# A second Strassen level in the fourth product of six projections

## The chip, the core and the metric

The kernel runs on one core of one Trainium2 chip. The metric is the device time of the launch in microseconds. The times below are of single executions; the profile is of one further execution, taken by the hardware profiler. Engines are named as the profile names them: PE (TensorE, matmuls), PEld (its weight loads), DVE (VectorE), ACT (ScalarE), POOL (GpSimd), SP (SyncE, which issues all DMAs here).

## What is computed

Four graph-attention layers over 128 graphs of 64 nodes with 512 features, all in float32. Each layer normalizes its input, applies a ReLU and adds the result of an attention whose mask is an adjacency matrix that all graphs share:

```python
h = jnp.maximum(_layernorm(x, axis=-1), 0.0)
x = x + layer(h)
# layer 0: softmax(q k^T / 8 + mask) v, q, k, v = h @ W + b, 8 heads of 64
# layer 1: the same, then @ Wo + bo
# layer 2: one head; (adj^T * (q k^T)), rows divided by their norm, times v; no bias
# layer 3: as layer 1 with one w_qkv, a projection w_proj, and o + layernorm(o) at its end
```

Nearly all of the arithmetic is in products of a 512x512 weight matrix with a block of activations.

## The kernel before

The 8192 rows (128 graphs x 64 nodes) are cut into 16 blocks of 512 rows (`T`), so each projection of a block is a product of two 512x512 matrices. The layers run one after another, and inside a layer the blocks. A block of layer 0 has three projections (q, k, v), of layer 1 four (q, k, v and the output projection o), of layer 2 two (two weight matrices are first folded into one by `fold`), of layer 3 four. The o projection of a block runs at the end of the next block (`pending`, `project`), when its attention is done.

**A projection.** Each one uses Strassen's form in Winograd's variant: the matrices are cut into 2x2 blocks of 256x256, and 7 block products stand for 8. `projection` (line 533) runs the products in the order of `ORDER` (line 44: 1, 6, 5, 2, 7, 3, 4). A product is four matmuls with a 128x128 stationary operand and 256 moving columns (`prod_T` for transposed results, with the weights stationary; `prod_N` with the activations stationary). A matmul of the code is two instructions in the trace[...]. The products accumulate in three PSUM banks of 512 columns (1 and 2; 6 and 7; 5 and 3), and product 4 has a bank of its own. Between products ACT and DVE copy parts out: `s1` (product 1), `u2` and `u3` (products 6 and 7 plus `s1`), `z5`. The four quarters of the result are written by:

- Y11: ACT copies the bank of products 1 and 2.
- Y12: DVE adds the bank of 5 and 3 to `u2`.
- Y22: POOL adds `u3` and `z5`.
- Y21: DVE adds the bank of product 4 to `u3`; with a bias it does so in two halves.

For the o projection of layer 1 (`emit_out1`) the residual rows `xo` take the place of `u2` and `u3`; POOL adds these into `xo`, and DVE adds the banks.

**Sums.** The sums of the activations' blocks that the products need (`S` for q, k and v; `SO` for o) are four additions of 128x512 on POOL (`sums_x`, line 501), for the very first block on DVE. The sums of the weights' blocks (`sums_w`) are made once for each weight matrix, on POOL, those of k0 on DVE.

**Attention.** `attend` issues the scores of a block (trace: so<-kT,qT) as one group of 64x64 matmuls, adds masks and takes maxima on DVE, subtracts on POOL, exponentiates on ACT, sums on DVE, normalizes on POOL, and transposes the weights by DVE copy, DMA transpose and ACT copy (tiles z, hp, s). Then follows the product with v (so<-s,v in layers 1 and 3, so<-v,s in layer 0), whose result goes in layer 1 to `oT` by DVE, from which `SO` is summed.

**The order of work.** The kernel records all operations first. `Plan` notes what each reads and writes and a duration for it (`duration`), and `order` (line 133) then makes a fixed order for each engine by list scheduling: each engine takes the ready step with the lowest rank, which is the order of recording. All products of a group (`plan.begin` to `plan.end`) stay together. Recording itself interleaves the work: projections are generators that stop after each product, and at each stop (`tick`) the due generators for attention, normalization, loads and stores go on by one step. So a product group is also the unit of time by which `yield` counts. All recorded instructions are issued from one line (L193 in the trace). On the chip each engine works through its own fixed list and waits where an input isn't there.

The buffers that the change touches: PSUM has four banks for the projections (`ps_mm`, trace: mm) and two tiles for attention (`ps_so`, trace: so), each handed out in turn by `Ring`; the weight tiles `w` hold 7 blocks of 256x256 for a matrix, four matrices at a time.

Of the kernel before, what the change touches and what calls it, by code (L numbers as in the profile page):

```python
# [18 lines left out]
P = 128  # L19
G = 64  # L20
# [23 lines left out]
ORDER = (1, 6, 5, 2, 7, 3, 4)  # L44
ORDER0 = (1, 2, 5, 6, 3, 7, 4)
# [172 lines left out]

PORT = 150.5
RUSH = 60  # L220
# [39 lines left out]
def gnn_stack_kernel(  # L260
# [26 lines left out]
    ps_mm = pool("ps_mm", 4, space=bass.MemoryType.PSUM)  # L287
    ps_so = pool("ps_so", 2, space=bass.MemoryType.PSUM)
# [10 lines left out]
    pw = ps_mm.tile([P, KC, P], F32, tag="mm", name="pw")  # L299
# [41 lines left out]

    def load_w(name, src):

        w = wp.tile([P, 7, 2, H2], F32, tag="w", name=name)


        def part(i, j):
            return src[i * H2 : (i + 1) * H2, j * H2 : (j + 1) * H2].rearrange("(c p) f -> p c f", p=P)

        dma(w[:, W11], part(0, 0))  # L350
        dma(w[:, W21], part(1, 0))
        dma(w[:, WT3], part(0, 1))
        dma(w[:, W22], part(1, 1))
        return w

    def sums_w(w, eng):
        tt = eng.tensor_tensor
        tt(w[:, WT1], w[:, WT3], w[:, W11], ALU.subtract)
        tt(w[:, WT2], w[:, W22], w[:, WT1], ALU.subtract)
        yield 1  # L360
        tt(w[:, WT4], w[:, W21], w[:, WT2], ALU.subtract)
        tt(w[:, WT3], w[:, W22], w[:, WT3], ALU.subtract)

    W = {}

    def weight(name, src, eng=gps):
        W[name] = load_w(name, src)
        yield 4
        yield from sums_w(W[name], eng)
# [27 lines left out]
    def raw(tag, src, nm):  # L397
        t = p1.tile([P, KC, D], F32, tag=tag, name=nm)
        for c in range(KC):
            dma(t[:, c, :], src[c * P : (c + 1) * P, :])  # L400
            yield 3
        return t

    def fold():

        rq = yield from raw("oT", wq2, "rq")
        rk = yield from raw("SO", wk2, "rk")
        yield 4
        for dc in range(KC):
            pa = ps_mm.tile([P, D], F32, tag="mm", name=f"pfa_{dc}")  # L410
            plan.begin()
            for ec in range(KC):
                pe.matmul(pa, rq[:, ec, ts(dc, P)], rk[:, ec, :], start=(ec == 0), stop=(ec == KC - 1))
            plan.end()
            f = p4.tile([P, D], F32, tag="z", name=f"fa_{dc}")
            act.copy(f, pa)
            yield 1
            dma(a2d[dc * P : (dc + 1) * P, :], f)
            yield 1
        rv = yield from raw("oT", wv2, "rv")  # L420
        yield 4
        for ec in range(KC):
            f = p4.tile([P, KC, P], F32, tag="z", name=f"ft_{ec}")
            turn(f, rv[:, ec, :], f"v2_{ec}")
            yield 1
            dma(v2d.rearrange("(c p) e -> p c e", p=P)[:, :, ts(ec, P)], f)
            yield 1
# [17 lines left out]
    hTs, Ss, vs = {}, {}, {}  # L445
    ready = set()
# [12 lines left out]
    def layer_norm(n):  # L459
        mv = sm.tile([P, NT, 2], F32, tag="mv", name=f"mv_{n}")  # L460
        rs = sm.tile([P, NT], F32, tag="rs", name=f"rs_{n}")
        nb = sm.tile([P, NT], F32, tag="nb", name=f"nb_{n}")

        def scales(at):
            pow_mhalf(rs[:, at], mv[:, at, 1], LN_EPS, f"{n}")
            dve.scalar_tensor_tensor(nb[:, at], mv[:, at, 0], -1.0, rs[:, at], ALU.mult, ALU.mult)

        for t in range(NT):
            stats(mv, t, xins[n][t], f"{n}")
            if n == 0:  # L470
                scales(slice(t, t + 1))
            if t % 2:
                yield 1
        if n:
            scales(slice(0, NT))
        yield 2
        hT = p2.tile([P, KC, T], F32, tag="hT", name=f"hT_{n}")
        hTs[n] = hT
        if n == 0:
            for t in range(NT):  # L480
                z = xins[n][t]
                act.activation(z, z, AF.Relu, bias=nb[:, t : t + 1], scale=rs[:, t : t + 1])
                pt = ps_mm.tile([P, KC, P], F32, tag="mm", name=f"pz_{n}_{t}")
                plan.begin()
                for c in range(KC):
                    pe.transpose(pt[:, c, :], z[:, ts(c, P)], ident)
                plan.end()
                if t == 1:
                    for i in range(WARM // 2):
                        pe.transpose(pw[:, i % KC, :], xins[n][0][:, ts(i % KC, P)], ident)  # L490
                (dve.tensor_copy if t else act.copy)(hT[:, :, ts(t, P)], pt)
        for t in range(NT) if n else ():
            z = xins[n][t]
            act.activation(z, z, AF.Relu, bias=nb[:, t : t + 1], scale=rs[:, t : t + 1])
            turn(hT[:, :, ts(t, P)], z, f"{n}_{t}")
            yield 1
        del xins[n]
        ready.add(("h", n))
        sums_of(n)

    def sums_x(tag, src, nm, eng):
        S = (p2 if tag == "S" else p1).tile([P, 4, 2, H2], F32, tag=tag, name=nm)
        x11, x12, x21, x22 = halves(src)
        tt = eng.tensor_tensor
        tt(S[:, 0], x21, x22, ALU.add)
        tt(S[:, 1], S[:, 0], x11, ALU.subtract)
        tt(S[:, 2], x11, x21, ALU.subtract)
        tt(S[:, 3], x12, S[:, 1], ALU.subtract)
        return {1: x11, 2: x12, 3: S[:, 3], 4: x22, 5: S[:, 0], 6: S[:, 1], 7: S[:, 2]}
# [19 lines left out]

    def projection(prod, w, xop, nm, emit, order=ORDER):  # L530

# [3 lines left out]
        def bank(i):  # L535
            banks[i] = ps_mm.tile([P, D], F32, tag="mm", name=f"pp{i}_{nm}")
            return banks[i]
# [5 lines left out]
        X = {1: 1, 2: 1, 6: 6, 7: 6, 5: 5, 3: 5, 4: 4}  # L543
        for i in order:
# [4 lines left out]
            prod(ps, w[:, BLOCKS[i]], xop()[i], first)  # L549
# [10 lines left out]
            elif i == 7:  # L560
                dve.tensor_tensor(tmp_tile("u3"), ps, tmp["s1"], ALU.add)
                emit("u3", tmp["u3"])
                emit("Y22", tmp["u3"], tmp["z5"])
            elif i == 4:
                emit("Y21", ps, tmp["u3"])
            elif i == 3:
                emit("Y12", ps, tmp["u2"])
            if i != order[-1]:
# [4 lines left out]
    def emit_plain(region):  # L573

        def emit(what, a, b=None):
# [15 lines left out]
    def emit_bias(region, bias):  # L591

        def emit(what, a, b=None):
# [37 lines left out]
    def scores(qT, kT, g, nm):  # L631
# [3 lines left out]
        pss = ps_so.tile([P, 2, 2, KC, G], F32, tag="so", name=f"pss_{nm}")  # L635
# [10 lines left out]
    def attend(n, qT, kT, v, done):  # L646
# [7 lines left out]
        for s, pss in zip(ss, psss):  # L654
            for b in range(2):
# [3 lines left out]
                )  # L659
            sf = s.rearrange("p q b j -> p (q b) j")  # L660
# [16 lines left out]
        for s in ss:  # L677
            aT = s.rearrange("p (q c) b j -> p q c (b j)", q=2)
            aTs.append(aT)
            for p in range(2):  # L680
                if n < N - 1:
                    turn(aT[:, p], s[:, p * KC : (p + 1) * KC].rearrange("p c b j -> p (c b j)"), f"a_{n}_{p}")
                else:
                    pt = ps_mm.tile([P, KC, P], F32, tag="mm", name=f"pa_{n}_{p}")
# [4 lines left out]
                    act.copy(aT[:, p], pt)  # L689
                yield 1  # L690
# [41 lines left out]
    def finish0(n):  # L732
        def done(aTs, v):
# [5 lines left out]
            for g, aT in enumerate(aTs):  # L739
                po = ps_so.tile([P, 2, 2, H2], F32, tag="so", name=f"po_{n}_{g}")  # L740
# [13 lines left out]
            for g, po in enumerate(pos):  # L754
                for j in range(2):
                    xv = xos[n][:, 2 * g : 2 * g + 2, j * H2 : (j + 1) * H2]
                    dve.tensor_tensor(xv, po[:, j], xv, ALU.add)
            yield 1
# [5 lines left out]
    def finish13(n):  # L764
        def done(aTs, v):
# [5 lines left out]
            for g, aT in enumerate(aTs):  # L771
                po = ps_so.tile([P, 2, 2, KC, G], F32, tag="so", name=f"po_{n}_{g}")
# [12 lines left out]
            for g, po in enumerate(pos):  # L785
                for b in range(2):
# [5 lines left out]
                    else:  # L792
                        act.copy(at, po[:, b])
            if n < N - 1:
                yield 1
                SOs[n] = sums_x("SO", oTs[n], f"SO_{n}", gps)
        return done

    def emit_out1(n):
# [3 lines left out]
        def emit(what, a, b=None):  # L803
# [18 lines left out]
    def emit_out3(n, o):  # L822
# [6 lines left out]
        def emit(what, a, b=None):  # L829
# [43 lines left out]
    def relate(n, hT=None, gT=None):  # L873


        prt = ps_mm.tile([P, D], F32, tag="mm", name=f"pr_{n}")
# [5 lines left out]
        if old:  # L882
# [6 lines left out]
            for g in range(2):  # L889
                po = ps_so.tile([P, 2, 2, H2], F32, tag="so", name=f"pv_{m}_{g}")  # L890
# [30 lines left out]
        if hT is not None:  # L921
            dve.tensor_tensor(rel, pr, adj2.unsqueeze(1).to_broadcast([P, NT, G]), ALU.mult)
            act.activation(sq, rel, AF.Square)
        yield 1
        if old:
            for t in range(NT):
                for j in range(2):
# [3 lines left out]
                    )  # L931
                yield t % 2
# [26 lines left out]
    def sums_of(n):  # L959
        assert ("h", n) in ready  # L960
        Ss[n] = sums_x("S", hTs[n], f"S_{n}", dve if n == 0 else gps)
# [3 lines left out]
    for name, got in zip(("q0", "k0"), first):  # L965
        W[name] = got
        now(sums_w(got, gps if name == "q0" else dve))
# [20 lines left out]
    def project(n):  # L988
# [5 lines left out]
        if m // NB == 1:  # L994
            run(projection(prod_N, W["o1"], sop, f"o_{m}", emit_out1(m)))
# [3 lines left out]
        else:  # L999
# [5 lines left out]
            run(projection(prod_N, W["o3"], sop, f"o_{m}", emit_out3(m, o)))  # L1005
            spawn(tail3(m, o))

    for n in range(N):
# [15 lines left out]
        if l != 2:  # L1024
            qT = p1.tile([P, KC, T], F32, tag="qT", name=f"qT_{n}")
            q_emit = emit_bias(region_T(qT), (bqc0, bqc1)[l]) if l < 2 else emit_plain(region_T(qT))
            run(projection(prod_T, W[f"q{l}"], xop, f"q_{n}", q_emit, ORDER if n else ORDER0))
# [4 lines left out]
            run(projection(prod_T, W[f"k{l}"], xop, f"k_{n}", k_emit))  # L1032
# [9 lines left out]
            run(projection(prod_N, W[f"v{l}"], xop, f"v_{n}", emit_plain(region_N(v))))  # L1042
# [3 lines left out]
        else:  # L1046
            gT = p1.tile([P, KC, T], F32, tag="qT", name=f"gT_{n}")
            run(projection(prod_T, W["a2"], xop, f"g_{n}", emit_plain(region_T(gT))))
# [5 lines left out]
            run(projection(prod_N, W["v2"], xop, f"v_{n}", emit_plain(region_N(v))))  # L1054
# [14 lines left out]
    for t in range(NT):  # L1069
        ps = ps_mm.tile([P, D], F32, tag="mm", name=f"pl_{t}")  # L1070
# [10 lines left out]
        dve.tensor_tensor(o, ps, R["bp"], ALU.add)  # L1081
        stats(mv, t, o, "last")
# [42 lines left out]
```

## Time and profile before

| | us |
|---|---|
| median of 3 runs | 2844.2 (2843.95 to 2844.62) |
| the profiled execution | 2844.57 |
| its span, first to last instruction | 2842.8 |

Shares of the stages, from the view of busy times by window:

| stage, us | PE | DVE | ACT | POOL |
|---|---|---|---|---|
| layer 0, 60 to 720 | 660.00 | 503.50 | 344.62 | 408.56 |
| layer 1, 740 to 1540 | 799.39 | 547.16 | 339.81 | 548.38 |

In a group's line of the profile stand line, engine, operation, output and inputs by the program's names (moving and stationary operand after the arrow), partitions and elements, the count, then the busy time in us and the mean duration in ns, then idle time before it and what ended that. Matmul records overlap: an instruction's record runs from its start to its last result, so spacing is read from the starts in the timeline. Each block of layer 1 takes 52.79 us (its scores start at 1063.42 us in one block and at 1169.01 us two blocks later).

### The profile page before, as it was taken

Reading aid. Unit: us, or ns where it says so; the run is one execution under the profiler, and the core shown is the slowest. Engines: PE = TensorE matmul, PEld = TensorE weight load, DVE = VectorE, ACT = ScalarE, POOL = GpSimd, SP = SyncE. Lnnn points to the kernel's source line nnn. Section 1 sums busy time; section 2 is a strip of 40 time slices with the busy share of each in tenths; the row PEclk is TensorE's granted clock in tenths of the full one; section 3 lists DMA queues with packets and bytes.
Section 4 is the critical chain, followed back from the end, with each engine's and each line's share of the span. In section 5 each row is a group of like instructions: output and inputs, shape, how many; then the busy total and the mean of one; then the engine's idle time right before and its main releaser. Section 6 shows DMA issues by size and latency. Waiting matters only on the chain.

```text
span 2842.8 us, 62036 instructions
## 1 busy us (share of the span) xinstructions
PE 2828.4 (99%) x25833; PEld 2471.6 (87%) x25833; DVE 2037.6 (72%) x3104; ACT 1248.0 (44%) x1589; POOL 1840.5 (65%) x1349
## 2 busy tenths in 40 slices
PE   9999999999999999999999999999999999999998
PEld 8878888888888888888888888888888888888887
DVE  7767778876767767667666555555688888778787
ACT  4555555454443534534434343443444444444442
POOL 6555566656766667667677334344678687787796
PEclk9999999999999999999999999999999999999999
DMA  6766666556453533533546565756433433433432
GB/s 158 163 137 156 143 146 134 127 128 163 105 120 80 124 95 82 131 85 86 136 114 156 136 162 143 164 128 157 120 86 94 119 86 95 112 91 96 109 84 66
DMA packets 634890, 342.29 MB, mean 120 GB/s; under 512 B 485232, under 2 KB 566384, under 8 KB 634608
## 3 DMA queue, kind: packets, MB, share of 16 engines
q1 hardware_dynamic: 634608, 338.32, 50.0%
q8 instruction: 202, 3.31, 0.5%
q14 instruction: 80, 0.66, 0.1%
HBM read 152.61 MB, written 69.21 MB: 78 GB/s over the span
## 4 chain that ended last, share of the span: by engine, by line
PE 96%; DVE 3%; issue 0%; POOL 0%; DMA 0%; ACT 0%; POOLq 0%; SPq 0%; DVEq 0%
PE mm L193 88%; PE so L193 8%; DVE z L193 1%; DVE st L193 0%; POOL s L193 0%; DVE u L193 0%; DVE sr L193 0%; DVE kT L193 0%; DMA xin<-in_x_dram 0%; DVE mv L193 0%; DVE w L193 0%; DVE xo L193 0%; ACT xin L193 0%; ACT oT L193 0%; POOLq L1120 0%
## 5 line engine op out<-in xcount | busy, mean ns | idle before, releaser
L193 PE MATMUL mm<-S,w 128*128 128x256 f32 x3584 | 817.2, 380 | 0.0
L193 PEld LDWEIGHTS mm<-S,w 128*128 128x128 f32 x3584 | 679.3, 190 | 93.8 <-issue 1.0
L193 PE MATMUL mm<-hT,w 128*128 128x256 f32 x2688 | 629.9, 380 | 4.0 <-DVE kT L193 3.7
L193 DVE TENSOR_TENSOR u<-mm,s 128x512 f32<-128x512 f32 x414 | 284.9, 688 | 480.1 <-PE mm L193 342.3
L193 PEld LDWEIGHTS mm<-hT,w 128*128 128x128 f32 x2688 | 509.6, 190 | 75.5 <-DVE kT L193 5.3
L193 PE MATMUL mm<-w,S 128*128 128x256 f32 x2048 | 472.8, 381 | 0.0
L193 PEld LDWEIGHTS mm<-w,S 128*128 128x128 f32 x2048 | 385.5, 190 | 53.8 <-issue 0.5
L193 ACT COPY hT<-hp 128x1024 uint16<-128x1024 uint16 x252 | 332.7, 1350 | 90.3 <-DMA hp<-z 90.2
L193 PE MATMUL mm<-w,hT 128*128 128x256 f32 x1536 | 366.4, 381 | 0.0
L193 ACT COPY s<-hp 128x1024 uint16<-128x1024 uint16 x188 | 252.3, 1352 | 204.3 <-DMA hp<-z 197.1
L193 ACT COPY s<-mm 128x512 f32<-128x512 f32 x211 | 123.0, 583 | 490.0 <-PE mm L193 419.0
L193 POOL TENSOR_TENSOR s<-s,mx 128x1024 f32<-128x1024 f32 x96 | 183.3, 1911 | 226.9 <-DVE mx L193 224.9
L193 PEld LDWEIGHTS mm<-w,hT 128*128 128x128 f32 x1536 | 289.2, 190 | 40.2 <-DVE v L193 0.2
L193 POOL TENSOR_TENSOR xo<-xo,row 128x512 f32<-128x512 f32 x192 | 286.1, 1510 | 8.4 <-DMA xo<-in_x_dram 5.7
L193 DVE COPY z<-s 128x1024 uint16<-128x1024 uint16 x188 | 278.2, 1501 | 6.7 <-POOL s L193 6.6
L193 DVE COPY z<-xin 128x1024 uint16<-128x1024 uint16 x252 | 245.3, 988 | 37.6 <-ACT xin L193 34.0
L193 ACT ACTIVATE xin<-xin,nb,rs 128x512 f32<-128x512 f32 x256 | 195.4, 808 | 90.5 <-DVE nb L193 89.9
L193 PE MATMUL mm<-w,SO 128*128 128x256 f32 x992 | 224.3, 379 | 0.0
L193 POOL TENSOR_TENSOR qT<-u,z 128x512 f32<-128x512 f32 x64 | 87.5, 1367 | 202.2 <-DVE u L193 189.8
L193 PEld LDWEIGHTS mm<-w,SO 128*128 128x128 f32 x992 | 188.5, 190 | 25.6
L193 POOL TENSOR_TENSOR s<-s,sr 128x1024 f32<-128x1024 f32 x96 | 187.3, 1963 | 34.2 <-DVE sr L193 32.1
L193 ACT ACTIVATE s<-s 128x1024 f32<-128x1024 f32 (+1 forms) x112 | 108.1, 966 | 200.3 <-POOL s L193 144.3
(98 smaller groups left out, 3667.7 us busy)
## 6 DMA issues: line engine op xcount, KB each, us to landing
xin<-x SPq DMA_DIRECT2D x192, 256.0 KB, 4.0
xo<-x SPq DMA_DIRECT2D x64, 512.0 KB, 4.5
xin<-in_x_dram SPq DMA_DIRECT2D x64, 256.0 KB, 3.2
x<-xo SPq DMA_DIRECT2D x64, 256.0 KB, 2.5
x<-xo SPq DMA_DIRECT2D x128, 128.0 KB, 2.5
x<-xo SPq DMA_DIRECT2D x32, 512.0 KB, 3.0
out_dram<-xo SPq DMA_DIRECT2D x30, 512.0 KB, 3.0
xo<-in_x_dram SPq DMA_DIRECT2D x32, 256.0 KB, 3.2
```

What stands on the lines that cost most here:

```text
L193: getattr(getattr(self.nc, eng), op)(*a, **k)
```

## The change

Product 4 multiplies the two blocks x22 and `WT4` as they are. In six projections (`LEVEL2`: k0 and v0 of layer 0, q1, k1, v1 and o1 of layer 1) it is now made by the same form once more: the 256x256 blocks are cut into 2x2 quarters of 128x128, and seven products of one 128x128 by 128x128 matmul stand for four of 128x256. They come in two groups, "4a" (four matmuls) and "4b" (three), in one bank, with the order of products 1, 6, 5, 4a, 2, 7, 3, 4b.

What belongs to it:

- `sums_x` makes four more sums of 128x128 where needed, into the place of x21, which nothing reads any more; `sums_w` makes four more for each of the six weight matrices, for which the weight tile is longer by 3 x 128 columns.
- After 4a ACT copies two quarters into a new tile `q` and DVE adds one; after 4b DVE adds another, and `close_2` writes the result with three POOL additions and two DVE ones, in place of the one addition of Y21.
- PSUM banks are now given and taken by name, in the order in which they come free (`Pool`), in place of the fixed turn of `Ring`. `fold` waits in recording until a bank is free, its loads are spread out (a stop of 12 for 3), and two stops in it are gone.

```diff
+FINER = (1, 6, 5, "4a", 2, 7, 3, "4b")
+LEVEL2 = {"k0", "v0", "q1", "k1", "v1", "o1"}
...
-    ps_mm = pool("ps_mm", 4, space=bass.MemoryType.PSUM)
-    ps_so = pool("ps_so", 2, space=bass.MemoryType.PSUM)
+    mm = ctx.enter_context(tc.tile_pool(name="ps_mm", bufs=1, space=bass.MemoryType.PSUM))
+    mm = Pool([mm.tile([P, D], F32, tag=f"mm_{i}", name=f"mm_{i}") for i in range(4)])
...
-        w = wp.tile([P, 7, 2, H2], F32, tag="w", name=name)
+        t = wp.tile([P, 7 * 2 * H2 + 3 * P], F32, tag="w", name=name)
...
+        t, e = w[:, WT4], W2[name]
+        if finer(name):
+            tt(e[:, 0], t[:, 0, P:], t[:, 0, :P], ALU.subtract)
+            tt(e[:, 1], t[:, 1, P:], e[:, 0], ALU.subtract)
+            yield 1
+            tt(e[:, 2], t[:, 1, :P], e[:, 1], ALU.subtract)
+            tt(t[:, 0, P:], t[:, 1, P:], t[:, 0, P:], ALU.subtract)
...
-            yield 3
+            yield 12
...
+        a, b, c, d = [x22[:, j, ts(i, P)] for i in range(2) for j in range(2)]
+        F = [x21[:, j, ts(i, P)] for i in range(2) for j in range(2)]
+        if needs2:
+            tt(F[0], c, d, ALU.add)
+            tt(F[1], F[0], a, ALU.subtract)
+            tt(F[2], a, c, ALU.subtract)
+            tt(F[3], b, F[1], ALU.subtract)
...
+    def prod_2(prod, ps, name, xop, todo):
...
+        at = {1: (0, 0), 2: (0, 0), 5: (0, 1), 3: (0, 1), 6: (1, 1), 7: (1, 1), 4: (1, 0)}
+        for i in todo:
+            x, out = xop["quarters"][i], quarter(ps, prod, *at[i])
+            a, b = (ws[i], x) if prod is prod_T else (x, ws[i])
+            pe.matmul(out, a, b, start=i == 1, stop=True, skip_group_check=True)
...
+    def close_2(prod, ps, q, base, dst, bias):
+        u2, u3, z5 = q[:, 1], q[:, 2], q[:, 3]
+        y12 = quarter(base, prod, 0, 1)
+        gps.tensor_tensor(y12, y12, u2, ALU.add)
+        y2 = base[:, :, P:] if prod is prod_T else base[:, 1, :].rearrange("p (v f) -> p v f", v=2)
+        gps.tensor_tensor(y2, y2, u3.unsqueeze(1).to_broadcast([P, 2, P]), ALU.add)
+        gps.tensor_tensor(dst[:, 1, P:], base[:, 1, P:], z5, ALU.add)
+        for at in ((slice(None), 0, slice(None)), (slice(None), 1, slice(0, P))):
+            if bias is None:
+                dve.tensor_tensor(dst[at], ps[at], base[at], ALU.add)
+            else:
+                dve.scalar_tensor_tensor(dst[at], ps[at], bias[at[1]], base[at], ALU.add, ALU.add)
...
+            elif i == "4a":
+                q = p1.tile([P, 4, P], F32, tag="q", name=f"q_{nm}")
+                act.copy(q[:, 0], quarter(pv, prod, 0, 0))
+                dst, base, bias = emit("close")
+                if bias is None:
+                    act.copy(q[:, 3], quarter(pv, prod, 0, 1))
+                else:
+                    act.activation(q[:, 3], quarter(pv, prod, 0, 1), AF.Identity, bias=bias[1])
+                dve.tensor_tensor(q[:, 1], quarter(pv, prod, 1, 1), q[:, 0], ALU.add)
+            elif i == "4b":
+                dve.tensor_tensor(q[:, 2], quarter(pv, prod, 1, 1), q[:, 0], ALU.add)
+                if base is None:
+                    base = tmp["u3"].rearrange("p (u v) -> p u v", u=2)
+                close_2(prod, pv, q, base, dst, bias)
```

## The prediction, made before the changed kernel ran

> **What bounds the kernel now.** I read the page's busy times and its chain first, then the matmul groups, then one block of the timeline.
>
> ```profile
> PE 2828.4 (99%) x25833; PEld 2471.6 (87%) x25833; DVE 2037.6 (72%) x3104; ACT 1248.0 (44%) x1589; POOL 1840.5 (65%) x1349
> ...
> PE 96%; DVE 3%; issue 0%; POOL 0%; DMA 0%; ACT 0%; POOLq 0%; SPq 0%; DVEq 0%
> ...
> L193 PE MATMUL mm<-hT,w 128*128 128x256 f32 x2688 | 629.9, 380 | 4.0 <-DVE kT L193 3.7
> L193 PEld LDWEIGHTS mm<-hT,w 128*128 128x128 f32 x2688 | 509.6, 190 | 75.5 <-DVE kT L193 5.3
> ```
>
> TensorE is on the chain for 96% of the span and hardly waits. Only PE time, or a new PE wait, can move the end. Inside layer 1 (740 to 1540 us) PE is busy 799.39 of 800 us, POOL 548.38, DVE 547.16: POOL has room, but not much.
>
> The timeline gives the true rate, as records overlap:
>
> ```profile
> 407.44 3.62 PE L193 MATMUL mm<-S,w 128*128 128x256 f32 x16
> ...
> 1565.55 2.08 PE L193 MATMUL mm<-qT,hT 128*64 128x64 f32 x64
> ```
>
> Sixteen 256-wide instructions last 3.62 us, the last one 0.38 alone: (3.62-0.38)/15 = 0.216 us each. A matmul of the code is two instructions, so a product of four is 8 x 0.216 = 1.726 us. In the second line, 64-column weights and 64-wide operands alternate between two halves of the array: (2.08-0.22)/63 = 29.5 ns, 59 ns per half.
>
> **What the Trainium skill says.** "TensorE: Matmul & The Clock Gate", section LDWEIGHTS: a load costs its columns / 1.2 GHz, 107 ns for 128. The trace agrees: after a pause at 12.1 us the first matmul's record is 483 ns where the others are 379, so it stood 104 ns behind its own load. Its section Back-to-back issue gap gives matmul streams with a load each a larger spacing at N=128 than the operand alone takes (81 ns for 56); no run here shows that for float32. "GPSIMD Engine Reference", section 3.1: a two-input add of 2048 takes 4497 ns, about 2.6 cycles an element, and section 1: its SBUF interfaces are shared with VectorE. The trace agrees with both:
>
> ```profile
> L193 POOL TENSOR_TENSOR xo<-xo,row x192: 1257/1712/1827, 34.9 to 2822.9; 128x512 f32<-128x512 f32 x192
> ...
> L193 POOL TENSOR_TENSOR S<-hT x126: 1254/1270/1731, 52.7 to 2748.6; 128x512 f32<-128x512 f32 x126
> ```
>
> Undisturbed 1.257 us for 512, and 1.71 when it meets VectorE.
>
> **The PE part.** The fourth product of six projections (k0, v0 in layer 0; q1, k1, v1, o1 in layer 1), 16 blocks each, is 96 products. Four 256-wide matmuls become seven 128-wide, 8 instructions become 14, each with its own load of 128 columns. The operand takes half of 256 wide: the 64-wide stream scaled up is 2 x 53 + 5 = 112 ns (59 ns is 53 of streaming and 5 beside), and the 104 ns load just fits behind it, as the 64-column loads already do behind 64-wide operands. So 14 x 0.112 = 1.568 us for 1.726: 0.158 us each, 96 x 0.158 = **15.2 us gained**. Bounds: 109 ns (half of 216 and nothing more) gains 19; at 123 ns (1.726/14) nothing is left; if loads blocked each other for their recorded 190 ns, 14 x 0.19 = 2.66 us would cost 90 us in all. The 59 ns stream speaks against that, since its loads are recorded at 138 ns and still don't space it.
>
> **VectorE and ScalarE.** The last add of the quarter (one of 512 wide at 685 ns, or two with bias at 478) becomes two 128-wide adds, one 256 and one 128. From 425 ns for 256 and 685 for 512 a 128-wide one is about 295: 295 x 2 + 425 + 295 = 1.31 us, so 0.46 to 0.63 us more. ScalarE gains two 128-wide copies, about 0.41 each (583 for 512, 471 for 256). In a layer-1 block of 52.8 us that is 2.2 us on VectorE (68% busy) and 3.3 us on ScalarE (42%). Both fit beside PE: cost 0, unless an add stands where PE waits for it (below).
>
> **POOL.** Each closing adds three operations (128, 256, 128 wide), and each sum of a layer-0 or layer-1 block, and of o1's input, four of 128. The trace has none so narrow. From 1.257 at 512 and 4.497 at 2048: 2.11 ns an element and 0.18 fixed, so 0.45 us for 128, 0.72 for 256. From below 0.31 (a quarter of 1.257), from above 0.90 (with the 0.45 that meeting VectorE adds). Per layer-1 block: 8 x 0.45 + 4 x 1.62 = 10.1 us, which takes POOL from 548/800 of 52.8 = 36.2 to 46.3 of 52.2 us, 89%. In layer 0, 1.8 + 3.24 = 5 us on top of 62%: room enough.
>
> **Where POOL meets PE.** The layer-1 block before:
>
> ```profile
> 1146.07 2.09 PE L193 MATMUL so<-s,v 64*64 64x64 f32 x128
> ...
> 1169.01 2.10 PE L193 MATMUL so<-kT,qT 64*64 64x64 f32 x128
> ```
> ```profile
> 1151.74 1.28 POOL L193 TENSOR_TENSOR SO<-oT 128x512 f32<-128x512 f32 x1 [3.06 <-DVE oT L193]
> 1153.10 1.27 POOL L193 TENSOR_TENSOR SO<-SO,oT 128x512 f32<-128x512 f32 x1
> ...
> 1161.80 1.26 POOL L193 TENSOR_TENSOR kT<-u,z 128x512 f32<-128x512 f32 x1
> ```
>
> After the attention product (so<-s,v) VectorE writes oT, POOL sums SO and S and then finishes k at 1163.1; scores start at 1169.0, so 5.9 us are spare. In the changed order of instructions scores stand after five products of v instead of three, and k's last part is now written by POOL, behind SO, its four small sums, S, four more, and its own closing. From the start of so<-s,v: PE needs 2.2 + 0.67 (rest of q's fourth) + six products 10.36 + 1.57 + five 8.63 = 23.4, and 1.05 more before the half of scores that reads the late part: 24.5 us. POOL: oT done 6.4 (5.67 before, and a small closing op now stands between its parts); SO 5.03, small 1.8, S 5.03, small 1.8, k 1.26, closing 1.62; nine handoffs between dependent small operations at 0.13 (1.36 between the starts above, where independent ones have 1.23) 1.2; 0.1 to PE: 24.2. Spare: 0.3 us.
>
> The other half, scores to the next so<-s,v: the last ScalarE copy of the weights ended at 1143.54, 27.4 us after that block's scores (1169.01 - 52.79 = 1116.22). A 1.7 us residual addition now stands before the second normalization on POOL: about +1.5, 28.9. PE arrives after 2.2 + 26.5 = 28.7. Spare: -0.2.
>
> Both are even to within about 1 us. What is queued behind such a wait is all of PE. I take **0.3 us a block, 15 blocks, 4.5 us lost**; bounds 0 and 2 us a block. In layer 0 k's closing stands ahead of the next block's sums on POOL, and scores follow 9.9 us of PE work later: 0. First block: four small sums on VectorE for the input and four for the weights of k0, about 8 x 0.3 us beside a PE that starts there: I take 0.7 us. Weights' small sums otherwise, PSUM banks handed out by name, and the spread-out loads in the fold lie beside PE work, no DMA is added: 0.
>
> **Sum.** -15.2 + 4.5 + 0.7 = -10.0 us. The profiled execution took 2844.57 (span 2842.8 and 1.8 around it), 0.4 above the median 2844.2; so **2834 us**, its own range 2825 to 2839.
>
> **Rivals.**
> Waits eat the gain: about 1 us a layer-1 block, 15 us; 2844. For it: two chains without spare. Against: PE waits nowhere in 60 to 720 or 740 to 1540 us now, apart from one 0.6.
> POOL's k chain sets layer 1's pace (slower): at 0.65 us per small operation, the eleven on the way to scores add 2.2 us, 1.9 beyond the spare: 15 x 1.9 = 28.5, less 15.2: 2857. It decides from 0.6 us an operation on. For it: short POOL operations have a fixed part that the trace shows badly (0.22 us for four elements at best, 0.42 on average). Against: POOL there runs at its undisturbed 1.26.
> Loads set the pace of 128-wide matmuls, at 130 ns: 14 x 0.13 = 1.82, 96 x 0.094 = +9 and the waits: 2858. Against: the 59 ns stream.
> The change doing nothing is excluded: the instructions differ.
>
> **How the numbers follow.** My forecast 0.58; waits eat it 0.18; POOL's pace 0.18; loads 0.06. The range 2824 to 2853 takes in 109 ns without waits at one end and most of the POOL case at the other. A change under 0.2% (5.7 us) can't be told from none. Faster 0.6 (with the mild end of the second case), same 0.16, slower 0.24.
>
> **What will show it.** 128-wide matmuls four in a row every 112 ns; closings of 0.45 and 0.72 us on POOL; in layer 1 PE waits for POOL or DVE kT at scores and for ACT s at so<-s,v of under 0.5 us a block, layer 0 none. A spacing above 120 ns, or waits above 1 us a block, makes me wrong.

## The result and the profile after

| | before | after |
|---|---|---|
| median of 14 runs each, us | 2844.31 (2843.69 to 2845.11) | 2850.29 (2847.81 to 2850.97) |
| the profiled execution, us | 2844.57 | 2850.78 |
| its span, us | 2842.8 | 2848.7 |

The changed kernel takes 1.002 of the time before, with an interval of 1.0012 to 1.0028: 6 us more, a fifth of a per cent; that is little, but the interval doesn't reach 1. The forecast was 10 us less. The same lines of the page as before, now of the changed kernel (busy us, share and instructions of each engine; the chain that ended last):

```profile
PE 2819.2 (99%) x26409; PEld 2475.3 (87%) x26409; DVE 2090.1 (73%) x3352; ACT 1284.5 (45%) x1781; POOL 2096.0 (74%) x1845
...
PE 88%; POOL 4%; DVE 4%; issue 1%; DMA 0%; ACT 0%; SPq 0%; POOLq 0%; DVEq 0%; ACTq 0%
```

PE's busy time fell by 9.2 us, but its share of the last chain fell from 96 to 88%: it now waits. The view of waits (engine, what it waited for, us in total, times, longest), first the longest line of the kernel before, then lines of the changed kernel:

```profile
PE mm L193 <- DVE kT L193: 3.7, 4, 0.9
```

```profile
PE mm L195 <- ACT z L195: 6.0, 5, 2.9
PE mm L195 <- DVE kT L195: 3.8, 4, 1.0
PE mm L195 <- ACT hT L195: 2.1, 1, 2.1
PE mm L195 <- ACT s L195: 1.7, 3, 0.7
PE mm L195 <- POOL S L195: 1.6, 3, 0.8
```

The wait for kT is as before. The others are new (for s it had been 0.2 us once), each a handful of long waits. They are not spread over the blocks. In the timeline of the changed kernel (start, us), scores of neighbouring layer-1 blocks start 52.14 us apart:

```profile
1075.91 2.09 PE L195 MATMUL so<-kT,qT 64*64 64x64 f32 x128
...
1106.62 2.66 PE L195 MATMUL mm<-hT,w 128*128 128x128 f32 x14
...
1128.05 2.10 PE L195 MATMUL so<-kT,qT 64*64 64x64 f32 x128
```

Before it was 52.79. A block gains 0.65 us, and that for every block from the scores at 1023.77 to those at 1440.88: four products, 0.163 us each. A block of layer 0 gains 0.33, two products. Ninety-six products would have brought 15.6 us.

To see where these went I took, for each pair of neighbouring projection matmuls, what the distance of their starts exceeds the usual one (0.216 us for 256 wide, 0.112 for 128), and summed it by place. In all it is 18.4 us before and 40.7 after, 22.3 more; less 15.6 that is 6.7, against 6.2 between the profiled executions. The places of the changed kernel where most of it stands (the kernel before loses under 2 us in all of them together):

| place, us | lost |
|---|---|
| end of the first block (42 to 56) | 5.1 |
| the fold begins (243 to 271) | 1.7 |
| layer 0 goes over to layer 1 (663 to 719) | 8.3 |
| second block of layer 1 (773 to 779) | 3.2 |
| next blocks of layer 1 (866 to 1003) | 2.5 |
| layer 1 goes over to layer 2 (1494 to 1584) | 3.1 |

**The seam between the layers.** The windows view gives the busy us of each engine from 655 to 735 us, before and after:

```profile
655.00:735.00 80.00, 80.00 (x843) 70.14 (x842) 59.93 (x91) 39.75 (x53) 52.69 (x38) 1.00 0.52 123
```

```profile
655.00:735.00 80.00, 73.78 (x837) 63.59 (x836) 57.66 (x96) 38.20 (x53) 71.64 (x73) 1.00 0.56 131
```

The columns are length, PE, PEld, DVE, ACT, POOL, clock, DMA share and GB/s. POOL went from 66 to 90%. PE lost 6.2 us here. In the timeline the longest wait of the kernel stands at 704.50:

```profile
694.95 2.35 POOL L195 TENSOR_TENSOR s<-s,sr 128x1024 f32<-128x1024 f32 x1
697.26 4.68 POOL L195 TENSOR_TENSOR w<-w 128x512 f32<-128x512 f32 x4
701.91 1.26 POOL L195 TENSOR_TENSOR qT<-u,z 128x512 f32<-128x512 f32 x1
...
702.41 1.34 ACT L195 COPY s<-hp 128x1024 uint16<-128x1024 uint16 x1 [2.10 <-DMA hp<-z]
703.62 0.83 ACT L195 ACTIVATE z<-mm,bk 128x256 f32<-128x256 f32 x2
...
704.50 1.99 PE L195 MATMUL mm<-S,w 128*128 128x256 f32 x8 [2.89 <-ACT z L195]
```

There is one z buffer (`z5`). It comes free when POOL has added u and z into q's Y22; that addition stands behind four large sums of the next weights and ends at 703.17. Then ACT writes the z of k, and only then may PE add product 3 to the same bank. ACT couldn't have done it before 703.6 either: its list has a copy of attention weights first, and that waited too, in the end for POOL's s<-s,sr. Both chains come out of POOL's list. Before, the same two stood behind only two of these sums, and with the other one first; POOL even waited half a microsecond between them:

```profile
682.72 2.65 POOL L193 TENSOR_TENSOR w<-w 128x512 f32<-128x512 f32 x2
685.32 1.28 POOL L193 TENSOR_TENSOR qT<-u,z 128x512 f32<-128x512 f32 x1
687.09 2.15 POOL L193 TENSOR_TENSOR s<-s,sr 128x1024 f32<-128x1024 f32 x1 [0.50 <-DVE sr L193]
```

So two things differ here: what POOL has to do, and the order that the planner makes of it.

**The first block.** Two lines of the timeline before, then the changed kernel's:

```profile
26.90 0.68 DVE L193 BATCH_NORM_STATS2 st<-xin 128x6 f32<-128x512 f32 x1
...
35.65 0.52 DVE L193 SCALAR_TENSOR_TENSOR nb<-mv,rs 128x4 f32<-128x4 f32 x1
```

```profile
27.44 3.45 DVE L195 TENSOR_TENSOR w<-w 128x128 f32<-128x128 f32 x3
...
32.41 0.68 DVE L195 BATCH_NORM_STATS2 st<-xin 128x6 f32<-128x512 f32 x1
...
39.05 1.12 DVE L195 SCALAR_TENSOR_TENSOR nb<-mv,rs 128x4 f32<-128x4 f32 x1
...
51.15 3.60 PE L195 MATMUL mm<-hT,w 128*128 128x256 f32 x8 [2.12 <-ACT hT L195]
```

Now three small weight sums of k0 take 3.45 us together on DVE, beside POOL's own weight sums, and stand ahead of the norm statistics: nb comes 3.4 us later than before, and PE waits 2.12 us for hT. Runs 9 and 14 below show that these sums are not the whole reason. And then PE runs at half its rate: the eight instructions that follow take 3.60 us where eight take 1.89 elsewhere, and in the window from 50 to 55 us the clock is 0.66:

```profile
50.00:55.00 5.00, 3.60 (x8) 2.35 (x8) 4.62 (x9) 3.38 (x4) 4.21 (x6) 0.66 0.68 205
```

### The profile page after: what moved, and what is told of

It is laid out like the page before. It is cut to its first block, busy times and chain, and to the rows that moved or that the text cites. A ratio compares the mean times of both kernels' runs of the same rounds, so it can differ in the third digit from the quotient of the medians.

```text
span 2848.7 us, 64374 instructions
## 1 busy us (share of the span) xinstructions
PE 2819.2 (99%) x26409; PEld 2475.3 (87%) x26409; DVE 2090.1 (73%) x3352; ACT 1284.5 (45%) x1781; POOL 2096.0 (74%) x1845
## 4 chain that ended last, share of the span: by engine, by line
PE 88%; POOL 4%; DVE 4%; issue 1%; DMA 0%; ACT 0%; SPq 0%; POOLq 0%; DVEq 0%; ACTq 0%
PE mm L195 81%; PE so L195 8%; DVE z L195 1%; POOL w L195 1%; POOL s L195 1%; POOL S L195 1%; DVE st L195 0%; DVE u L195 0%; POOL SO L195 0%; POOL u L195 0%; DVE sr L195 0%; POOL hT L195 0%; DVE xo L195 0%; DVE kT L195 0%; POOL v L195 0%
## 5 line engine op out<-in xcount | busy, mean ns | idle before, releaser
L195 PE MATMUL mm<-hT,w 128*128 128x256 f32 (+1 forms) x2976 | 628.7, 357 | 9.6 <-DVE kT L195 3.8
L195 PEld LDWEIGHTS mm<-hT,w 128*128 128x128 f32 x2976 | 517.1, 191 | 75.9 <-DVE kT L195 5.4
L195 PE MATMUL mm<-w,hT 128*128 128x256 f32 (+1 forms) x1728 | 363.7, 354 | 1.1 <-ACT kT L195 0.9
L195 PEld LDWEIGHTS mm<-w,hT 128*128 128x128 f32 x1728 | 296.0, 190 | 36.4 <-ACT kT L195 1.3
L195 DVE COPY z<-xin 128x1024 uint16<-128x1024 uint16 x252 | 260.8, 1052 | 16.1 <-ACT xin L195 14.7
L195 POOL TENSOR_TENSOR S<-hT 128x512 f32<-128x512 f32 x126 | 161.6, 1283 | 78.7 <-ACT hT L195 78.6
L195 POOL TENSOR_TENSOR s<-s,sr 128x1024 f32<-128x1024 f32 x96 | 196.1, 2046 | 5.3 <-DVE sr L195 4.4
```

Source lines behind the costliest of these rows:

```text
L195: getattr(getattr(self.nc, eng), op)(*a, **k)
```

## The experiments

My first theory, A: the added POOL work is too much where a layer begins. Rivals: B, the banks by name and the fold (no part of the new arithmetic) reorder the work; C, the planner takes POOL's small operations for shorter than they are, and so its order is poor. One thing bears on all runs: the planner orders the work anew for each version, so an edit changes the operations and the order together. The times below are medians with their ranges, the ratios to the kernel before, run beside each version, with their intervals. "Seam" means the stretch in which one layer goes over to the next.

**1. No second level at all**, with banks and fold as changed.

```diff
-LEVEL2 = {"k0", "v0", "q1", "k1", "v1", "o1"}
+LEVEL2 = set()
```

> The changed kernel with no projection in the second level (LEVEL2 empty): what stays is PSUM banks by name and the fold's other stops. Theory A (the loss comes from the second level's own small operations, which crowd POOL and VectorE at the seams: first block, layer 0 to 1, layer 1 to 2): as before, 2844.3 within 1 us. Theory B (the loss of some 21 us comes from the banks by name and the fold): 2850 or more, up to 2865. In between: the fold alone would show as about 1.5 us near 260 us.

Measured: 2844.5 us (2843.77 to 2845.53), 1.0 (0.9992 to 1.0009). The excess of the matmuls is 18.5 us, as before the change. B falls; all of the loss belongs to the second level.

**2 and 3. One layer alone**: `LEVEL2 = {"k0", "v0"}`, and `LEVEL2 = {"q1", "k1", "v1", "o1"}`.

> Second level for k0 and v0 alone. Gain 32 x 0.163 = 5.2 us. Theory A: the stall of the first block (5.0 us lost near 50 us) and near 260 us (1.5) stay, the seam to layer 1 keeps a small part: 2846 to 2848. Theory B: 21 lost without the rest of the gain, 2860.

> Second level for q1, k1, v1, o1 alone. Gain 64 x 0.163 = 10.4 us. Theory A: no stall near 50 us, the seams at 660 to 790, 866 to 1002 and 1495 to 1584 us stay (some 15 us): 2847 to 2850. Theory B: 21 lost, 2855.

Layer 0 alone: 2850.35 us (2849.41 to 2852.12), 1.0022 (1.0013 to 1.003). Missed: 32 products lose as much as all 96. Its trace loses 3.3 us in the first block, 1.7 at the fold and 4.9 at the seam. Layer 1 alone: 2849.25 us (2847.32 to 2850.59), 1.0017 (1.0011 to 1.0024); the first block and the fold are clean, the seam loses 3.8 and the second block of layer 1 3.2. Both layers load the seam from their side.

**4. Without the small weight sums.** They are left out, and quarters of `WT4` stand in for them, so the six projections compute something else.

```diff
-            tt(e[:, 0], t[:, 0, P:], t[:, 0, :P], ALU.subtract)
...
-            tt(t[:, 0, P:], t[:, 1, P:], t[:, 0, P:], ALU.subtract)
...
-        ws = {1: w[:, 0, :P], 2: w[:, 1, :P], 3: w[:, 1, P:], 4: e[:, 2], 5: e[:, 0], 6: e[:, 1], 7: w[:, 0, P:]}
+        ws = {1: w[:, 0, :P], 2: w[:, 1, :P], 3: w[:, 1, P:], 4: w[:, 0, P:], 5: w[:, 0, P:], 6: w[:, 1, P:], 7: w[:, 0, P:]}
```

> The second level in all six, but the four small sums of each weight matrix are left out and quarters of WT4 stand in for them, so the product 4 of these projections is computed from other operands. If the small weight sums on POOL and VectorE are what fills the seams: of 21 us lost some 13 go, 2836 to 2839. Rival: the small sums of S and the closings do it, and the weight sums are 24 operations too few to matter: 2847 to 2850.

Measured: 2850.41 us (2848.23 to 2854.42). The first block loses 2.2 us instead of 5.1; of these 2.9 us some 1.5 are the stretch at half rate, which is absent here. Between 667 and 781 us the loss is 14.6, some 1.7 of it in a stretch at half clock that begins at 777 us; the changed kernel has 11.6. So nothing is gained there with fewer operations. The small weight sums are not what is too much there.

**5. Longer POOL durations in the plan** for fewer than 512 elements.

```diff
-        return n * (1.82 if n > D else 2.41), 120
+        return (n * 1.82 if n > D else n * 2.41 if n == D else 220 + 2.03 * n), 120
```

> The changed kernel, but the plan that orders the work counts 220 ns + 2.03 ns an element for a POOL operation under 512 wide (480 for 128) where it counted 308 for 128; the operations are the same. Theory C (the order is made for a POOL that is faster than it is, so at the seams operations stand too late in the queues): the loss of some 21 us is halved or better, 2833 to 2840. Theory D (POOL and VectorE are simply full at the seams, and no order helps): 2849 to 2852.

Measured: 2852.44 us (2850.38 to 2854.3), 1.0029 (1.0017 to 1.004), 2 us more than with the shorter durations. C falls in the form that this run gives it: these durations don't help the changed kernel. (The profiled execution has three stretches at half clock, where that of the changed kernel has one, so part of the 2 us may be chance.) That a better order would help is not excluded.

**6 to 8. The second level from the third block of each layer on** (`LO = 2`), the same with the durations of run 5, and from the fourth block on (`LO = 3`). The small weight sums run in the block before.

```diff
-    def finer(name):
-        return name in LEVEL2
+    def finer(name, n):
+        return name in LEVEL2 and n % NB >= LO
...
+    def later(name, n):
+        if name in LEVEL2 and n % NB == LO - 1:
+            spawn(sums_2(name), 1)
```

> The second level only from the third block of layer 0 and of layer 1 on, its small weight sums made in the second block. 6 x 14 = 84 products gain 84 x 0.163 = 13.7 us. If the loss belongs to second-level work in the first blocks of a layer: of 21 us lost the first block's 5 and most of the seam's 11 go, some 5 us stay (fold, end of layer 1): 2834 to 2838. If the stalls only move to where the second level begins: 2845 or more.

> Both: second level from the third block on and the longer POOL durations in the plan. Theory C: a little better than without the durations, 2831 to 2835. Theory D: the same as without, 2834 to 2838.

> Second level from the fourth block on: 78 products, 12.7 us gained. If two blocks suffice to be clear of the seams: 1 us above the run from the third block. If the seams reach further: at or below it.

From the third block: 2839.92 us (2837.64 to 2840.58), 0.9984 (0.9977 to 0.999); with the durations 2837.44 (2836.77 to 2838.3), 0.9976 (0.9967 to 0.9985); from the fourth 2838.87 (2837.85 to 2839.83). Run 6 has twelve products fewer and takes 10 us less than with all, still 2 us more than I expected at most; run 8 is no slower than run 6 with six products fewer still. The seam's window in run 6:

```profile
655.00:735.00 80.00, 79.28 (x845) 69.26 (x844) 58.92 (x93) 40.30 (x54) 62.11 (x55) 1.00 0.53 130
```

POOL is at 78% and PE misses 0.7 us instead of 6.2. This shows that the second level in the first two blocks is what costs. It does not show what in those blocks does it, as products, sums and closings left them together. The order counts too: run 7 has the operations of run 6, and in the same 80 us POOL is busy 68.15 and PE misses 3.2, though the whole is faster.

**9 to 12. The sums early; the durations alone; both refinements.** Run 9 is run 6 with the small weight sums at the arrival of the weights. Run 10 is run 1 with the durations of run 5. Run 11 is run 8 with them. Run 12 has the second level from the third to the fourteenth block, with these durations.

```diff
-        return name in LEVEL2 and n % NB >= LO
+        return name in LEVEL2 and LO <= n % NB < HI
...
+        elif name in LEVEL2 and n % NB == HI - 1:
+            t = W[name][:, WT4]
+            gps.tensor_tensor(t[:, 0, P:], t[:, 1, P:], t[:, 0, P:], ALU.subtract)
```

> As the second level from the third block on, except that three of the four small weight sums (and the third once more, so that there are four) run when the weights arrive, as in the changed kernel; only the sum made in place waits for the second block. 84 products. If the small weight sums, standing in POOL's queue at the seam, are what makes TensorE wait there, the stalls near 670 to 710 us come back and the time is 2847 or more. If it is the small additions of the fourth products in the blocks beside the seam (two a product more on POOL, and POOL's operations between S and the end), the seam keeps the 1 to 2 us that it lost with the sums moved, and only the first block loses its 3 to 5 us again, since the sums of k0 are back on VectorE there: 2842 to 2845.

> No second level at all, but the planner counts POOL's operations of fewer than 512 elements as 220 + 2.03 n ns. If the 2.5 us by which these durations bettered the version from the third block belong to the second level's small operations, nothing is gained here: 2843.5 to 2845. If they belong to the older operations of 256 elements (the additions on half tiles, also in the kernel before), then 2841 to 2843 here, and the comparison of the second level with the kernel before has to be made against this time.

> Second level from the fourth block on, with the longer POOL durations. 78 products at 0.162 us give 12.6 us. If only the places beside a seam lose, the losses left are those of the version from the third block less what its third block cost: 2836 to 2838, no different from it or up to 1 us better. If every product that is taken back is simply 0.16 us lost: 2838.5.

> Second level in the third to the fourteenth block of layers 0 and 1 only, so both sides of each seam are plain: 24 + 48 = 72 products, 11.7 us at 0.162 us; the sum made in place is undone after the fourteenth block (the same subtraction again). If all of the loss sits in the blocks beside the seams, nothing is lost and the time is 2832 to 2834, better than the version from the third block though it has 12 products fewer. If the losses near 668 to 684 us come from the seam's own work (the next weights and their large sums), 12 products less only cost 1.9 us: 2838 to 2840.

Run 9: 2839.56 us (2838.41 to 2842.21), as run 6 and under both ranges that I had named: the small weight sums cost nothing that can be told here. The first block hardly loses either (0.8 us), though k0's sums are back on DVE; so in the changed kernel, where it loses 5.1, they do so only together with the other work of the second level. Run 10: 2844.52 us, 1.0001 (0.9993 to 1.0009): without a second level the durations change nothing; they helped runs 7 and 11, and not run 5. Run 11 is the best version of all: **2835.54 us (2835.36 to 2837.27), 0.9971 (0.996 to 0.9983)**. Its page and its waits:

```profile
PE 94%; DVE 3%; POOL 2%; issue 1%; ACT 0%; DMA 0%; POOLq 0%; SPq 0%; DVEq 0%
```

```profile
PE mm L195 <- ACT z L195: 1.6, 1, 1.6
...
PE mm L195 <- DVE u L195: 1.2, 2, 1.1
```

PE is busy for all of the 80 us from 655 to 735 there, and two long new waits are left, one for u near 767 us and one for z near 1508. Run 12, with 72 products: 2837.22 us (2836.35 to 2838.35). I expected 2832 to 2834; its excess is 21.1 us, 2.7 over before, with 1.2 at 668 and 1.3 at 854. So some loss is left at the seam though both of its sides are plain; what it belongs to isn't shown.

**13 to 15. POOL's part put back alone.** Run 6, with the small sums of S and SO made in the first two blocks too (13), with three small POOL additions behind each of their projections, on buffers that nothing reads any more (14), and with both (15); the products there stay plain.

```diff
+            if i == order[-1] and name in LEVEL2 and i != "4b":
+                y, z = tmp["u3"].rearrange("p (u v) -> p u v", u=2), tmp["z5"]
+                gps.tensor_tensor(y[:, 0, P:], y[:, 0, P:], z[:, :P], ALU.add)
+                gps.tensor_tensor(y[:, :, P:], y[:, :, P:], z[:, P : 2 * P].unsqueeze(1).to_broadcast([P, 2, P]), ALU.add)
+                gps.tensor_tensor(y[:, 1, :P], y[:, 1, P:], z[:, 2 * P : 3 * P], ALU.add)
```

> As the second level from the third block on, with the four small sums of S and of SO made in every block of layers 0 and 1 (of SO in layer 1 only), so also in the first two, where nothing reads them. If POOL's time at the seams is the cause and its part ahead of the products weighs most (the sums stand between the last hT and what follows S in POOL's queue): 2843 to 2846. If POOL's closings weigh most, or the cause is not POOL's time: 2839 to 2841.5.

> As the second level from the third block on, with three small POOL additions (128, 256 and 128 elements wide, on buffers that nothing reads any more) behind each of the named projections of the first two blocks, as a finer product's closing has them. If POOL's time at the seams is the cause and the closings weigh most: 2843 to 2847. If the sums of S do, or the cause is not POOL's time: 2839 to 2841.5.

> Both: the small sums of S and SO and the three closing additions in the first two blocks, with plain products there. If POOL's time at the seams is the cause: 2846 to 2850, near the changed kernel. If it is something else in the finer products (ACT's copies, VectorE's additions, the planner's order of the pieces): under 2843.

| | us | over run 6 |
|---|---|---|
| 13, sums | 2840.21 (2839.17 to 2841.34) | 0.3 |
| 14, closings | 2848.1 (2846.37 to 2850.24) | 8.2 |
| 15, both | 2851.45 (2848.98 to 2855.62) | 11.5 |

The closings alone bring 8.2 us back, and with the sums it is 11.5, of some 12 that all 96 products cost over run 6 (10.4 in time, and 2.0 that the twelve products should have gained). The sums alone bring nothing. Both times with closings lie a little above what I had expected. In run 14 the losses stand at several places: in the first block (3.1 us, where run 6 has 0.2 and run 13 too), from 655 to 785 us (6.0, where run 6 has 1.6), at 839 and 865 us (2.7), and 1.6 at 444 us, in the middle of layer 0, where nothing was added. Its timeline at the seam, near the same place:

```profile
695.98 3.40 POOL L195 TENSOR_TENSOR w<-w 128x512 f32<-128x512 f32 x2
699.33 2.56 POOL L195 TENSOR_TENSOR u<-u,z 128x128 f32<-128x128 f32 x3
...
701.59 0.86 DVE L195 COPY z<-xin 128x1024 uint16<-128x1024 uint16 x1 [0.71 <-DMA hp<-z]
702.37 0.68 DVE L195 TENSOR_TENSOR u<-mm,s 128x512 f32<-128x512 f32 x1
...
703.10 1.13 PE L195 MATMUL mm<-w,S 128*128 128x256 f32 x4 [2.27 <-DVE u L195]
```

The three additions stand behind two weight sums and hold u until 701.89; DVE writes the next u at 702.37, when a copy that waited for a transposing DMA is done as well. Here too several chains end together, half a microsecond apart, so no single one of these waits is the cause. What is shown is what set them off: adding 36 POOL operations of 0.64 us on average, in the first two blocks of the two layers, costs 8.2 us. Whether it is their time or the other order that the planner makes with them isn't separated: POOL's list at the seam has another order than in run 6, and nothing was added near the loss at 444 us. The order alone moved the time by 2.5 us between runs 6 and 7 and by 3.3 between runs 8 and 11.

**16 to 18. The closings on DVE**: in the changed kernel with all 96 products, for the first two blocks of the two layers (16; 12 products and 36 additions, not the 14 and 42 that the expectation names), with the durations of run 5 (17), and for all blocks (18).

```diff
+        eng = dve if k < 2 else gps
...
-        gps.tensor_tensor(y12, y12, u2, ALU.add)
+        eng.tensor_tensor(y12, y12, u2, ALU.add)
```

> The changed kernel with all of its 96 finer products; only the three closing additions of the first two blocks of layers 0 and 1 are on VectorE instead of POOL (42 additions, 14 products). If POOL's time in these blocks is the cause, most of the 10 us comes back: 2838 to 2843; the first block's loss stays (VectorE's small weight sums of k0 are still there, and now its closings too). If the finer product as such makes the loss (ACT's and VectorE's additions, the order of the pieces): 2847 to 2851.

> The same with the planner's longer durations for POOL's operations under 512 elements. They bettered the version from the third block by 2.5 us, and the version from the fourth by 3.3, and did nothing for the changed kernel, whose POOL queue was full at the seam. With the seam relieved: 1 to 3 us under the run before it. If they do nothing: the same as it.

> The closings of all 96 products on VectorE. If VectorE has room in every block (53.6 of 80 us in a steady stretch of layer 1, to which four closings of some 1.1 us a block add 6 us), this is as the first of these runs or 1 to 3 us better, since the end of layer 1, where POOL was busy 49 of 50 us, is relieved too: 2836 to 2842. If VectorE's chain to the softmax takes the delay instead: over 2845.

16: 2853.22 us (2852.61 to 2855.19), 1.0033 (1.0021 to 1.0045); 17: 2852.7 us (2851.45 to 2854.95); 18: 2896.07 us (2891.65 to 2896.87), 1.0179 (1.0165 to 1.0193). None gained, though I had expected it: run 16 lies above even the range for the case that the finer product as such makes the loss, run 17 can't be told from it, and run 18 is far slower. The seam in run 16:

```profile
655.00:735.00 80.00, 74.22 (x846) 64.25 (x845) 62.62 (x106) 41.75 (x60) 69.69 (x68) 1.00 0.57 134
```

POOL has 2 us less to do there, DVE 5 us more, and PE misses 5.8 us, now over half of it waiting for POOL's S. By itself this speaks against POOL's time as the cause, or for another order that costs as much; the run can't tell them apart. In run 18 each steady block of layer 1 takes 55.03 to 56.75 us, 2.2 to 4.0 more than in the kernel before. Its timeline:

```profile
1035.66 1.81 POOL L195 TENSOR_TENSOR hT<-hT 128x128 f32<-128x128 f32 x4
1037.43 1.26 POOL L195 TENSOR_TENSOR kT<-u,z 128x512 f32<-128x512 f32 x1
...
1038.73 0.29 DVE L195 TENSOR_TENSOR u<-u,q 128x128 f32<-128x128 f32 x1 [4.93 <-POOL kT L195]
...
1039.37 1.99 PE L195 MATMUL mm<-w,S 128*128 128x256 f32 x8 [2.65 <-ACT z L195]
```

PE waits for the z of v, and DVE, with all of its work behind it, for the same addition of POOL, which stands behind the sums of SO and S. The Trainium skill ("TensorE: Matmul & The Clock Gate", section "Architectural detail: the array is 16× 32×32, not 1× 128×128") calls VectorE a strict first-in-first-out queue; this trace agrees as far as it goes: nothing ran on it in those 4.93 us, though whether a later operation was ready isn't shown. POOL is not late by itself: from so<-s,v to the end of this addition it takes 18.7 us (1019.94 to 1038.69), in the changed kernel 21.0. But PE comes to the last of v's products with a sum 16.8 us after so<-s,v, where the changed kernel has 26.5 us of work in between (1104.60 to 1131.07). With other engines for the closings the planner makes another order, and in run 18 a worse one. So 16 to 18 show no gain from the move; how much room DVE has they don't tell.

## Why the prediction was wrong

Point by point:

- **The PE part, 0.158 us a product: right.** Fourteen instructions 128 wide follow each other every 0.112 us in the median, and a steady block gains 0.163 us a product. The weight loads don't set the pace.
- **POOL's small operations, 0.45 and 0.72 us: nearly right.** In the sums of S and SO 128 wide takes 0.46 us, in the closings 0.46 to 0.54; 256 wide takes 0.75 to 0.78. The by-form groups of the changed kernel (busy us, mean ns of one):

```profile
L195 POOL TENSOR_TENSOR u<-u,q 128x256 f32<-128x256 f32 x80 | 60.1, 751 | 14.8 <-DVE q L195 14.0 <-ACT hT L195 0.8
L195 POOL TENSOR_TENSOR hT<-hT 128x128 f32<-128x128 f32 x124 | 55.1, 465 | 2.4
L195 POOL TENSOR_TENSOR u<-u,q 128x128 f32<-128x128 f32 x80 | 42.8, 536 | 7.0 <-DVE q L195 4.5
...
L195 DVE TENSOR_TENSOR w<-w 128x128 f32<-128x128 f32 x4 | 4.8, 1210 | 0.0
```

  The rival in which POOL's chain sets layer 1's pace needed 0.6 us, and so falls. Two readings behind the estimate were too wide. No addition of 2048 was run here, so no trace confirms the figure for it. And 1.71 us "when it meets VectorE" is not what a 512-wide addition takes beside any VectorE work: in the kernel before 110 of the 126 S additions ran beside some, and only two took over 1.5 us.
- **Layer 1's two chains, 4.5 us lost: nothing was lost at these chains.** From so<-s,v to the scores PE needs 23.45 us (1104.60 to 1128.05), where I had 23.4 to the start; POOL finishes k 22.8 us after so<-s,v, where I had 24.1. From 860 to 1480 us PE waits 1.4 us in all, and none of it for scores or so<-s,v, with POOL busy 533.81 of 620 us, 86% (I had 89).
- **The first block, 0.7 us: 5.1** in the profiled execution. The prediction counted DVE's small sums alone. Those of k0's weights took 1.21 us each, not 0.3, while POOL worked beside them; yet with plain products they lose only 0.8 (run 9). POOL's closings, which had no term here, bring the loss to 3.1 by themselves (run 14; 0.2 without them in run 6). And some 1.5 us are the matmuls at half rate after the pause of 2.12 us, which not every such pause brings (run 18, below).
- **The step that failed** is the one that took the rest at nothing: "In layer 0 k's closing stands ahead ...: 0", with POOL's "5 us on top of 62%: room enough", and "Weights' small sums otherwise ... lie beside PE work, no DMA is added: 0". I worked out POOL's added work for a steady block and an average block, not for the blocks where a layer begins, where POOL's list also holds the weights' large sums. The losses came to 22.3 us, where the sum had 5.2. Adding POOL's small operations in the first two blocks of the two layers costs 11.5 us by runs 6 and 15, mostly through the closings (8.2, run 14); the small weight sums, which I named, hardly cost anything by themselves (run 9). That the added operations do it is shown; how much of it is their time on POOL, and how much the order that the planner then makes, stays open. With that step at 0 the sum was bound to come out as a gain.
- "Waits eat the gain" (2844) had the kind of loss right, but its place and its size wrong: not 1 us in each layer-1 block but about 20 us, mostly at the beginnings and ends of layers.

The wide range, 2824 to 2853, held the result near its upper end, but by luck: it was drawn that high for slow small operations on POOL, which didn't come. The forecast's own range, 2825 to 2839, didn't hold it. What stays open: which of POOL's neighbours at the seam has to move for all 96 products to pay. What PE waits for differs between versions (z in the changed kernel, u in run 14, S in run 16); common to them is a POOL list that is full from 660 to 710 us: busy for 47.4, 45.9 and 46.4 of these 50 us, where the kernel before has 31.8 and run 6 35.8. Why taking 2 us off it (run 16) doesn't help is open too. A second z buffer, or the large weight sums earlier, was not tried. That the share of 90% as such is too much isn't shown: 86% in the steady blocks costs nothing.

## What to carry to other kernels

Work the added load of a helper engine out for the worst stretch, not for the mean or the steady one: where a layer begins, the next weights' preparation shares its list, and here several waits of other engines led back to that one list. If a change pays in steady blocks and loses at the seams, leave it out at the seams; here 18 of 96 products fewer, and truer durations in the plan, turned 6 us lost into 9 us won. And where a planner makes the order, moving an operation to another engine moves everything: judge it by a run, not by that engine's free time.

## What the runs showed of the hardware

A pause of 2.12 us on PE (49.03 to 51.15) was followed by 256-wide instructions 0.427 us apart, twice the usual 0.216, and a mean clock of 0.66 from 50 to 55 us; after the longer pause of 2.89 us at 704.50 eight took 1.99 us, the full rate. The Trainium skill ("TensorE: Matmul & The Clock Gate", section "What's actually happening") lets the rate fall after an idle window of about 3.4 us, free-running; the trace shows that less idle time than that can do, and that the length of the pause doesn't decide alone. Run 18 shows this best: in twelve places of layer 1 PE pauses for 2.63 to 2.66 us, and five of these pauses go with a stretch of 3.41 us at half clock, the other seven don't. A 128-wide addition with both inputs in SBUF took 0.27 to 0.29 us on DVE in all 91 cases of run 18 in which POOL was idle meanwhile (0.28 at 1008.12 us), and 0.28 to 1.67, 1.10 in the median, in the 60 in which POOL worked throughout (1.21 at 1002.34 us).
